# The end of a post-norm layer: order of the last tiles, low rank product apart from its transposition, last norm on POOL

## The chip, the cores and the metric

The kernel runs on one core of one Trainium2 chip. The metric is the device time of one execution in microseconds (us); lower is better. Times of the profile are counted from the start of its span. PE is the matrix engine, PEld its weight loads, DVE the vector engine, ACT the activation engine, POOL the general engine, SP the engine that issues most DMAs.

## What is computed

One transformer layer with a norm behind each half, in float32, on 2 sequences of 512 tokens and 512 channels:

```python
x = _layernorm(x + attention(x, Wq, bq, Wk, bk, Wv, bv, Wo, bo))   # 32 heads, 8 groups, D = 128, RoPE, causal softmax
x = _layernorm(x + ffn(x, ...))

def ffn(x):
    y = einsum('bth,oh->bto', x, W_base) + b_base
    z = einsum('bth,erh->bter', x, lora_A[active])                 # 4 active experts of rank 8
    contribs = einsum('bter,eor->bteo', z, lora_B[active]) * 2.0
    logits = (einsum('bth,eh->bte', x, router_W) + router_b)[..., active]
    alpha = softmax(log(domain_prior[active] + 1e-12) + logits)
    return y + einsum('bteo,bte->bto', contribs, alpha)
```

## The kernel before

The order of every instruction is written out by hand: each engine works through its own queue in the order in which the program names the instructions, and waits there for whatever an instruction needs from another engine. Attention is cut into 16 units (8 groups times 2 sequences) and each unit into four blocks of 128 query rows, which are `parts` 0 to 63. The function `slot(T)` is called once for every step T; four steps make the scores of one part. In step T stand the score of step T, the context product (`weigh`) of an earlier step, softmax steps of the three scores before, the transposition of probabilities on DVE (`blocks_transposed`), their way through DRAM (`blocks_out`, then `blocks_in` two parts later, both on SP's queue), and then whatever `put(T, ...)` has hung on that step. A context product of part p stands in step 4p + 12 (`LAG_CTX`), and ACT copies its sum out of the one PSUM bank `ctx` one step after the last (`context_out`). The output product (`wo_mm`, four heads) and `wo_out`, which adds it to the residual `x_sb`, follow.

The last 19 steps and what stands behind them also hold the second half of the layer. Its eight tiles of 128 tokens are objects of the class `Ffn`: `f0` are the four tiles of the first sequence (`fz` is the last of them), `fa` two tiles of the second, `fb` the third and `fc` the fourth. The last unit's parts come in the order 2, 3, 0, 1, so that parts 62 and 63 are short ones. A tile goes through these steps:

- `stats`, `root`, `centre`: the first norm (DVE, then Sqrt on ACT and a reciprocal on DVE, then DVE);
- `transpose`: four PE transposes into a bank `tp` and an ACT copy to `x1T`;
- `base`: x times W_base in two banks, with the low rank and router columns in the same products (4 times `base(c)`, 16 instructions); for fc, `route` does the router columns alone, 16 columns wide, and `half` the two halves of the base product later;
- `logits`, `alphas`: softmax over four experts (DVE, Exp on ACT, DVE), ending in `zs`;
- `low_rank`: PE transposes `zs` into `tz`, DVE copies that to `zT`; `finish`: PE multiplies `zT` (33 rows) with `bmT` into the base product's banks, DVE adds the residual and takes the statistics of the second norm;
- `store`: the second norm is applied (`Norm.apply`, a tensor_scalar on DVE) and SP issues the store. fc is added on PE (`ident` times x) and stored in two halves, on SP's and ACT's queue.

E is the step after the last score (256) and A is 245. The banks are QX and QY for f0[0], f0[1], fz and fb; SC and SC for f0[2], fa[0] and fc; WX and WY for fa[1]; CTX serves the contexts and some transposes; `tz` has a bank of its own.

Of the kernel before, what the change touches and what calls it, by code (L numbers as in the profile page):

```python
# [9 lines left out]
F32 = mybir.dt.float32  # L10
# [5 lines left out]
P = 128  # L16
# [13 lines left out]
def postln_layer_kernel(  # L30
# [33 lines left out]
    nc = tc.nc  # L64
    B, S, HID = x.shape
    NT = B * S // P
    TPB = S // P
    KC = HID // P
# [470 lines left out]
    def weigh(p, j):  # L539
        u, i = parts[p]  # L540
        g, b = unit(u)
        if j == 0:
            psc[p] = ps_ctx.tile([P, R, P], F32, tag="ctx", name="pc")
        nc.tensor.matmul(  # L544
            psc[p], lhsT=v_sb[g // VG, b * TPB + j][:, ts(g % VG, D)], rhs=pT[p][:, :, ts(j, P)],
            start=(j == 0), stop=(j == i))

    def context_out(p):
        ctxT[p] = work.tile([P, R, P], F32, tag="ctxT", name=f"ctxT_{p}", bufs=3)
        nc.scalar.copy(ctxT[p], psc[p])  # L550
# [73 lines left out]
    class Norm:  # L624
# [4 lines left out]
            self.rstd = pool.tile([P, n], F32, name=f"rstd_{name}")  # L629
            self.pool = pool  # L630

        def stats(self, i, *srcs):

            st = self.pool.tile([P, len(srcs), 6], F32, tag=f"st{len(srcs)}", name="st", bufs=2)
            for k, src in enumerate(srcs):
                nc.vector.bn_stats(st[:, k, :], src)  # L636
            nc.vector.bn_aggr(self.mv[:, i, :], st)

        def root(self, lo, hi):
            nc.scalar.activation(self.rstd[:, lo:hi], self.mv[:, lo:hi, 1], AF.Sqrt, bias=eps_sb)  # L640
            nc.vector.reciprocal(self.rstd[:, lo:hi], self.rstd[:, lo:hi])

        def apply(self, i, dst, src=None):
            nc.vector.tensor_scalar(
                dst, dst if src is None else src, self.mv[:, i, 0:1], self.rstd[:, i : i + 1], ALU.subtract, ALU.mult)

    class Ffn:
# [28 lines left out]
        def base(self, c):  # L676
            if c == 0:
                self.new_banks()
            for n in range(2):
                w = OH + (ARH, WX_COLS - OH)[n]  # L680
                nc.tensor.matmul(  # L681
                    self.py[n][:, :w], lhsT=self.xT[:, c, :], rhs=wbT[:, c, n, :w], start=(c == 0), stop=(c == KC - 1),
                    skip_group_check=True)
# [40 lines left out]
        def finish(self):  # L724
            for n in range(2):
                nc.tensor.matmul(  # L726
                    self.py[n][:, :OH], lhsT=self.zT, rhs=bmT[:, ts(n, OH)], start=False, stop=True,
                    skip_group_check=True)
            for n in range(2):
                nc.vector.tensor_tensor(self.y[:, ts(n, OH)], self.py[n][:, :OH], self.x[:, ts(n, OH)], ALU.add)  # L730
            self.norm2.stats(self.i, self.y)

        def half(self, n):

            if n == 0:
                self.py = [pool.tile([P, OH], F32, tag=tag, name="ph") for pool, tag in self.banks]
            py = self.py[n]
            for c in range(KC):
                nc.tensor.matmul(py, lhsT=self.xT[:, c, :], rhs=wbT[:, c, n, :OH], start=(c == 0), stop=False)
            nc.tensor.matmul(py, lhsT=ident, rhs=self.x[:, ts(n, OH)], start=False, stop=False)  # L740
            nc.tensor.matmul(py, lhsT=self.zT, rhs=bmT[:, ts(n, OH)], start=False, stop=True)

        def store(self):
            self.norm2.apply(self.i, self.y)
            nc.sync.dma_start(out=outf[ts(self.t, P), :], in_=self.y)

        def store_halves(self):
# [15 lines left out]
    def put(slot, f):  # L763
        extra.setdefault(slot, []).append(f)
# [46 lines left out]
            put(wo_from(set_units(n)[0]) - 1 + k, lambda n=n, k=k: wo_sums(n, k))  # L811


    plain_at = {}
    free = LAST + LAG_WO + 1
    for p in range(NP - 2 * TPB, NP):
# [5 lines left out]
    def slot(T):  # L822

        uq, step = divmod(T + 24, UNIT)
        kq, step = divmod(step, 8)
        now = B <= uq < NU
        if now and step != 7 and step != 4:
            q_products(uq, kq, {0: 2, 1: 6, 2: 5, 3: 7, 5: 4, 6: 3}[step])
        un, kn = (uq, 1) if kq == 0 else (uq + 1, 0)
        if B <= un < NU and step == 7:  # L830
            q_products(un, kn, 1)
        plain_q = T - T_BEGIN < UNIT and divmod(T - T_BEGIN, QB)
        if plain_q:
            r, c = plain_q
            q_mm(1, r, c, *q_banks[r])
        uk, l = divmod(T + UNIT, UNIT)
        if 0 < uk < NU and l < KC:
            k_mm(uk, l)

        gv, tv = divmod(2 * (uk - 3) + (l >= 11), NT)  # L840
        gv += 1
        new_v = 0 < gv < G // VG and (gv > 1 or tv >= 3)
        if new_v and l in (7, 8, 11, 12):
            for c in range(2):
                v_mm(gv, tv, 2 * (l in (8, 12)) + c, ps_k, "k")
        kw, sw = divmod(T - LAG_WO, 8)
        products = 0 <= kw < LAST // 8
        if products:
            wo_products(kw, sw)
        plain = plain_at.get(T)  # L850
        if plain:
            p, step_o = plain
            wo_mm(p, 2 * step_o)
            wo_mm(p, 2 * step_o + 1)
        if 0 <= T < T_END:
            score(T)
        pc, j = divmod(T - LAG_CTX, QB)
        if 0 <= pc < NP and j <= parts[pc][1]:
            weigh(pc, j)

        if now and step in (0, 2, 4, 6):
            q_copy(uq, kq, ("p1", "u2", "u3", "c21")[step // 2])
        pc, j = divmod(T - 1 - LAG_CTX, QB)
        if 0 <= pc < NP and j == parts[pc][1]:
            context_out(pc)

        if 0 <= T - 3 < T_END:
            normalise(T - 3)
        if 0 <= T - 1 < T_END:
            masked_max(T - 1)  # L870
            exponentials(T - 1)
        if products:
            wo_adds(kw, sw)
        if sw == 0 and 0 < kw <= LAST // 8:
            wo_adds(kw - 1, 8)
        if now and step in (1, 5, 7):
            q_sum(uq, kq, {1: 0, 5: 2, 7: 3}[step])
        if 0 <= T - 2 < T_END:
            reciprocals(T - 2)
        if 0 <= T - 4 < T_END:  # L880
            blocks_transposed(T - 4)
            if (T - 4) % QB == QB - 1:
                blocks_out((T - 4) // QB)
        if T % QB == 1 and 0 <= T // QB - 2 < NP:
            blocks_in(T // QB - 2)
        if 0 <= (T - LAG_WO + 1) // 8 < LAST // 8 and (T - LAG_WO + 1) % 8 == 0:
            ctx_sums((T - LAG_WO + 1) // 8)

        ur, sr = divmod(T + 24 - 7, UNIT)
        kr, sr = divmod(sr, 8)  # L890
        if B <= ur < NU and sr < 6:
            q_rope(ur, 2 * kr + (sr < 3), sr % 3)
        r, part = divmod(T - T_BEGIN - QB, QB)
        if 0 <= r < R and part < 3:
            q_rope(1, r, part)
        if 0 < uk < NU and l in (KC, KC + 1, KC + 2):
            k_rope(uk, l - KC)
        if new_v and l in (10, 14):
            v_out(gv, tv)
        if plain and step_o:  # L900
            wo_out(p)
        for f in extra.pop(T, ()):
            f()
# [74 lines left out]
    for k, f in enumerate(f0):  # L978
        put(A + (-7, -6, 0, 0)[k], f.stats)
        put(A + 1 + k // 2, f.centre)  # L980
        put(A + 3 + k // 2, lambda f=f, k=k: f.transpose(*(QX, QY)[k % 2]))
        at = A + (5, 10, 12, 100)[k]
        for c in range(KC):
            put(at + c // 2, lambda f=f, c=c: f.base(c))
        put(at + 2, lambda f=f: (f.logits(), f.alphas()))
        put(at + 3, lambda f=f: (f.low_rank(), f.finish()))
    put(A + 15, lambda: (f0[0].norm2.root(0, 3), [f.store() for f in f0[:3]]))
    put(E + 2, fa[0].stats)
    for T in range(T_PROJ, E + 7):
        slot(T)  # L990


    fz = f0[3]
# [6 lines left out]
    fa[0].norm1.root(0, 2)  # L1000
    for f in fa:
        f.centre()
    for r in range(R):
        wo_mm(NP - 2, r)
    wo_out(NP - 2)
    for j in range(2):
        weigh(NP - 1, j)
    context_out(NP - 1)
    base(fz)
    fb.stats()  # L1010
    fb.norm1.root(0, 1)
    fb.centre()
    for f in fa:
        f.transpose(*SC)
    for r in range(R):
        wo_mm(NP - 1, r)
    wo_out(NP - 1)
    fc.stats()
    fc.norm1.root(0, 1)
    fc.centre()  # L1020
    fz.logits()
    fz.alphas()
    base(fa[0])
    fb.transpose(*CTX)
    fz.low_rank()
    fz.finish()
    fa[0].logits()
    fa[0].alphas()
    base(fa[1])
    fc.transpose(*CTX)  # L1030
    fa[0].low_rank()
    fa[0].finish()
    fc.route(*CTX)
    fc.logits()
    fc.alphas()
    fa[1].logits()
    fa[1].alphas()
    base(fb)
    fc.low_rank()
    fa[1].low_rank()  # L1040
    fa[1].finish()
    fb.logits()
    fb.alphas()
    fz.norm2.root(3, 4)
    fz.store()
    fc.half(0)
    fa[0].norm2.root(0, 2)
    for f in fa:
        f.store()
    fb.low_rank()  # L1050
    fb.finish()
    fc.half(1)
    fb.norm2.root(0, 1)
    fb.store()
    fc.norm2.stats(0, *fc.py)
    fc.norm2.root(0, 1)
    fc.store_halves()

# [49 lines left out]
```

## Time and profile before

| | |
|---|---|
| median of 3 runs | 850.36 us (848.46 to 852.32) |
| the profiled execution | 850.84 us, span 849.1 us |
| mean granted PE clock | 0.993 |
| PE busy | 831.3 us, 98% of the span |
| DVE, ACT, POOL busy | 599.9, 347.2, 277.3 us |
| chain that ended last | PE 91%, DVE 5%, ACT, DMA, issue and POOL 1% each |
| last score product starts | 770.08 us |
| last PE product ends, last store issued | 843.98, 846.28 us |

In the rows of the timeline the first number is the start, the second the time on the engine, then come engine, line, operation, tiles written and read, their shapes and how many instructions were merged; in brackets stands how long the engine was idle before, and who released it. A float32 product counts as two instructions.

### The profile page before, as it was taken

How to read it: one execution, taken by the hardware profiler on the slowest of the kernel's cores; microseconds unless marked ns; L12 is line 12 of the kernel's file. 1: busy time of each engine (PE TensorE's matmuls, PEld its weight loads, DVE VectorE, ACT ScalarE, POOL GpSimd, SP SyncE). 2: the span in 40 equal slices, each digit the busy share in tenths (PEclk: the TensorE clock that was granted, in tenths of full speed). 3: DMA queues.
4: the chain of work that ended last, by engine and by line, in shares of the span. 5: the costliest groups of instructions: out<-in, count | busy, mean ns of one | idle time of the engine just before them, and what ended most of it. 6: DMA issues, size and time to landing. Idle time of an engine off the chain costs nothing.

```text
span 849.1 us, 10726 instructions
## 1 busy us (share of the span) xinstructions
PE 831.3 (98%) x3201; PEld 587.0 (69%) x3201; DVE 599.9 (71%) x1970; ACT 347.2 (41%) x996; POOL 277.3 (33%) x312
## 2 busy tenths in 40 slices
PE   9999999999999999999999999999999999999895
PEld 5567767777777777777777777777777776555463
DVE  5478977787757877686768777787768779654444
ACT  1225454535444453444343453435343445651221
POOL 6463334233332234233422134353432424000000
PEclk9999999999999999999999999999999999999997
DMA  9026536462744455462634555463626445771201
GB/s 292 31 66 190 159 97 192 106 195 71 199 112 125 149 160 157 102 192 69 195 100 126 164 159 151 134 205 84 187 77 187 136 116 166 221 218 49 86 1 62
DMA packets 84971, 116.47 MB, mean 137 GB/s; under 512 B 6581, under 2 KB 64797, under 8 KB 82866
## 3 DMA queue, kind: packets, MB, share of 16 engines
q1 hardware_dynamic: 84258, 115.50, 47.6%
q0 software_dynamic: 448, 0.14, 0.2%
q8 instruction: 25, 0.41, 0.2%
q14 instruction: 32, 0.26, 0.1%
q10 hardware_dynamic: 208, 0.15, 0.1%
HBM read 71.73 MB, written 44.04 MB: 136 GB/s over the span
## 4 chain that ended last, share of the span: by engine, by line
PE 91%; DVE 5%; ACT 1%; DMA 1%; issue 1%; POOL 1%; DVEq 0%; SPq 0%; POOLq 0%
PE pc L544 16%; PE sc L488 13%; PE qx L429 11%; PE wx L429 11%; PE pp L355 9%; PE qy L429 8%; PE wy L429 8%; PE pv L342 7%; PE py L681 3%; PE po L615 2%; PE tp L274 1%; DMA pT<-db 1%; PE py L726 1%; DVE st L636 1%; DVE wt L568 0%
## 5 line engine op out<-in xcount | busy, mean ns | idle before, releaser
L503 ACT ACTIVATE p<-sc,nmax 128x288 f32<-128x288 f32 (+15 forms) x256 | 124.2, 485 | 254.1 <-DVE nmax L496 207.7
L496 DVE CUSTOM_DVE_ANT_0 sc<-sc,maskw 128x288 f32<-128x288 f32 (+15 forms) x256 | 114.2, 446 | 154.8 <-PE sc L488 152.1
L544 PE MATMUL pc<-pT,v 128*128 128x512 f32 x320 | 165.7, 600 | 2.2 <-DMA pT<-db 1.4
L488 PE MATMUL sc<-kT,qT 128*128 128x160 f32 (+15 forms) x512 | 161.9, 398 | 1.1 <-ACT p L503 1.1
L511 ACT ACTIVATE p<-p,den 128x288 f32<-128x288 f32 (+15 forms) x256 | 133.5, 521 | 0.1
L376 POOL TENSOR_TENSOR qT<-q,t 128x512 f32<-128x512 f32 x56 | 71.0, 1268 | 188.1 <-DVE q L375 188.1
L488 PEld LDWEIGHTS sc<-kT,qT 128*128 128x128 f32 x512 | 96.8, 190 | 30.5 <-issue 14.3
L416 POOL TENSOR_TENSOR cs<-ctxT 128x256 f32<-128x256 f32 x28 | 26.5, 946 | 196.2 <-PE wy L429 109.5
L550 ACT COPY ctxT<-pc 128x512 f32<-128x512 f32 x64 | 37.4, 585 | 121.0 <-PE pc L544 121.0
L519 DVE STREAM_TRANSPOSE zt<-p 128x128 f32<-128x128 f32 (+2 forms) x192 | 81.8, 426 | 0.0
L544 PEld LDWEIGHTS pc<-pT,v 128*128 128x128 f32 x320 | 56.9, 190 | 22.4 <-issue 5.3
L355 PE MATMUL pp<-xT,wk 128*128 128x512 f32 x128 | 65.0, 593 | 0.5 <-ACT xT L275 0.5
L342 PE MATMUL pv<-wv,xT 128*128 128x256 f32 x256 | 63.6, 379 | 0.0
L429 PE MATMUL wx<-wo,ctxT 128*128 128x256 f32 x224 | 57.7, 380 | 0.4 <-DVE den L507 0.4
L429 PE MATMUL qx<-xs,wq 128*128 128x256 f32 x224 | 58.0, 381 | 0.0
L342 PEld LDWEIGHTS pv<-wv,xT 128*128 128x128 f32 x256 | 48.5, 190 | 13.4 <-issue 7.1
L521 DVE STREAM_TRANSPOSE zt<-p 128x32 f32<-128x32 f32 (+3 forms) x256 | 57.6, 225 | 0.0
L429 PEld LDWEIGHTS qx<-xs,wq 128*128 128x128 f32 x224 | 41.4, 190 | 22.3 <-issue 16.0
L429 PEld LDWEIGHTS wx<-wo,ctxT 128*128 128x128 f32 x224 | 42.4, 190 | 13.5 <-issue 7.7
L503 ACT ACTIVATION_READ_ACCUMULATOR p<-sc,nmax 128x1 f32 x256 | 49.9, 195 | 0.0
L601 DVE TENSOR_TENSOR x_sb<-wx,x_sb 128x256 f32<-128x256 f32 x112 | 47.0, 419 | 0.0
L368 DVE SCALAR_TENSOR_TENSOR t<-q,bqkT,rope_sb 64x512 f32<-64x512 f32 x56 | 43.0, 768 | 1.3
(187 smaller groups left out, 1354.7 us busy)
## 6 DMA issues: line engine op xcount, KB each, us to landing
db<-zt SPq DMA_DIRECT2D x64, 256.0 KB, 4.1
pT<-db SPq DMA_DIRECT2D x16, 1024.0 KB, 4.8
db<-zt SPq DMA_DIRECT2D x64, 192.0 KB, 3.1
pT<-db SPq DMA_DIRECT2D x16, 768.0 KB, 4.4
wq<-in_L_attn_Wq_dram SPq DMA_DIRECT2D x20, 512.0 KB, 4.6
wo<-in_L_attn_Wo_dram SPq DMA_DIRECT2D x10, 1024.0 KB, 7.6
db<-zt SPq DMA_DIRECT2D x64, 128.0 KB, 2.4
pT<-db SPq DMA_DIRECT2D x16, 512.0 KB, 4.1
```

Source lines behind the costliest of these rows:

```text
L342: nc.tensor.matmul(psq["v", gg, t], lhsT=xT[:, c, ts(t, P)], rhs=wvs[gg][0][:, c, :], start=(c == 0), stop=(c == KC - 1))
L355: nc.tensor.matmul(psq[key], lhsT=wt[:, c, cols], rhs=xT[:, c, ts(b, S)], start=(c == 0), stop=(c == KC - 1))
L376: nc.gpsimd.tensor_tensor(dst, t1[:].rearrange("p (n s) -> p n s", s=BLK), t2[:].rearrange("p (n s) -> p n s", s=BLK), ALU.add)
L429: nc.tensor.matmul(ps, lhsT=wt[:, c, :], rhs=xt[:, c, :], start=start and c == 0, stop=c == CH - 1, skip_group_check=True)
L488: nc.tensor.matmul(sc[s][:, :w], lhsT=qT[u][:, i * QB + n].rearrange("p r s -> p (r s)"), rhs=kT[u][:].rearrange("p n s -> p (n s)")[:, :w ...
L496: nc.vector.tensor_tensor_reduce(sc[s][:, :w], sc[s][:, :w], maskw[:, S - w :], -SCALE, -MASKED, ALU.add, ALU.min, nmax[s])
L503: nc.scalar.activation(ptile[s][:, :w], sc[s][:, :w], AF.Exp, bias=nmax[s], scale=-1.0, accum_out=rden[s])
L511: nc.scalar.activation(ptile[s][:, :w], ptile[s][:, :w], AF.Copy, scale=rden[s])
L519: nc.vector.transpose(z[:, :, last - i : last, n, :].rearrange("p q j s -> p j q s"), ptile[s][:, : i * P])
L521: nc.vector.transpose(z[:, : n + 1, last, n, :], ptile[s][:, i * P : w])
L544: nc.tensor.matmul(psc[p], lhsT=v_sb[g // VG, b * TPB + j][:, ts(g % VG, D)], rhs=pT[p][:, :, ts(j, P)], start=(j == 0), stop=(j == i))
L601: nc.vector.tensor_tensor(into, pw[k, bank], into, ALU.add)
```

## The change

The change touches the last steps only. `low_rank` and `finish` of a tile are put apart, with other PE work between them, and `finish` is split into the product (`finish`) and the DVE part (`add`). `Norm.apply` takes an engine, and `store` uses POOL; fc's `store_halves` stays on DVE. Part 62's context product comes one step later, part 63's behind `base(fz)`. f0[1] and f0[2] start one step later, and the stores of f0[0] to f0[2] stand behind the steps. The two `half` products of fc are cut into single steps, between which fb's `finish` is placed, and fc's statistics are taken half by half. In the tail the order of the tiles' steps is another one.

```diff
-        def apply(self, i, dst, src=None):
-            nc.vector.tensor_scalar(
+        def apply(self, i, dst, src=None, engine=nc.vector):
+            engine.tensor_scalar(
                 dst, dst if src is None else src, self.mv[:, i, 0:1], self.rstd[:, i : i + 1], ALU.subtract, ALU.mult)
...
+        def add(self):
             for n in range(2):
                 nc.vector.tensor_tensor(self.y[:, ts(n, OH)], self.py[n][:, :OH], self.x[:, ts(n, OH)], ALU.add)
             self.norm2.stats(self.i, self.y)
...
+        def half(self, n, c):
+            if n == c == 0:
                 self.py = [pool.tile([P, OH], F32, tag=tag, name="ph") for pool, tag in self.banks]
+                self.st = self.own([P, 2, 6], "st")
+            nc.tensor.matmul(
+                self.py[n], lhsT=self.xT[:, c, :], rhs=wbT[:, c, n, :OH], start=(c == 0), stop=False)
+        def half_end(self, n):
             py = self.py[n]
-            for c in range(KC):
-                nc.tensor.matmul(py, lhsT=self.xT[:, c, :], rhs=wbT[:, c, n, :OH], start=(c == 0), stop=False)
             nc.tensor.matmul(py, lhsT=ident, rhs=self.x[:, ts(n, OH)], start=False, stop=False)
             nc.tensor.matmul(py, lhsT=self.zT, rhs=bmT[:, ts(n, OH)], start=False, stop=True)
+        def half_stats(self, n):
+            nc.vector.bn_stats(self.st[:, n, :], self.py[n])
+            if n:
+                nc.vector.bn_aggr(self.norm2.mv[:, self.i, :], self.st)
         def store(self):
-            self.norm2.apply(self.i, self.y)
+            self.norm2.apply(self.i, self.y, engine=nc.gpsimd)
             nc.sync.dma_start(out=outf[ts(self.t, P), :], in_=self.y)
...
+    weigh_at = {}
+    for p in range(NP - 1):
+        for j in range(parts[p][1] + 1):
+            weigh_at.setdefault(QB * p + LAG_CTX + j + (p == NP - 2), []).append((p, j))
...
-        at = A + (5, 10, 12, 100)[k]
+    for f, at in zip(f0, (A + 5, A + 11, A + 13)):
         for c in range(KC):
             put(at + c // 2, lambda f=f, c=c: f.base(c))
         put(at + 2, lambda f=f: (f.logits(), f.alphas()))
-        put(at + 3, lambda f=f: (f.low_rank(), f.finish()))
-    put(A + 15, lambda: (f0[0].norm2.root(0, 3), [f.store() for f in f0[:3]]))
+        put(at + 3, f.low_rank)
+        put(at + 4, lambda f=f: (f.finish(), f.add()))
...
     for f in fa:
         f.centre()
+    f0[0].norm2.root(0, 3)
+    for f in f0[:3]:
+        f.store()
     for r in range(R):
         wo_mm(NP - 2, r)
     wo_out(NP - 2)
-    for j in range(2):
-        weigh(NP - 1, j)
-    context_out(NP - 1)
     base(fz)
     fb.stats()
     fb.norm1.root(0, 1)
     fb.centre()
+    for j in range(2):
+        weigh(NP - 1, j)
+    context_out(NP - 1)
     for f in fa:
         f.transpose(*SC)
+    fb.transpose(*CTX)
+    fz.logits()
+    fz.alphas()
     for r in range(R):
         wo_mm(NP - 1, r)
     wo_out(NP - 1)
     fc.stats()
     fc.norm1.root(0, 1)
     fc.centre()
-    fz.logits()
-    fz.alphas()
+    fz.low_rank()
     base(fa[0])
-    fb.transpose(*CTX)
-    fz.low_rank()
-    fz.finish()
     fa[0].logits()
     fa[0].alphas()
+    fz.finish()
+    fc.transpose(*CTX)
+    fz.add()
     base(fa[1])
-    fc.transpose(*CTX)
     fa[0].low_rank()
-    fa[0].finish()
     fc.route(*CTX)
     fc.logits()
     fc.alphas()
     fa[1].logits()
     fa[1].alphas()
-    base(fb)
+    fa[0].finish()
+    fa[0].add()
+    fa[1].low_rank()
+    for c in range(KC):
+        fb.base(c)
+        if c == 1:
+            fa[1].finish()
+            fa[1].add()
     fc.low_rank()
-    fa[1].low_rank()
-    fa[1].finish()
+    fz.norm2.root(3, TPB)
+    fa[0].norm2.root(0, 2)
+    for f in (fz, *fa):
+        f.store()
     fb.logits()
     fb.alphas()
-    fz.norm2.root(3, 4)
-    fz.store()
-    fc.half(0)
-    fa[0].norm2.root(0, 2)
-    for f in fa:
-        f.store()
+    for c in range(KC):
+        fc.half(0, c)
+    fc.half_end(0)
+    fc.half_stats(0)
     fb.low_rank()
-    fb.finish()
-    fc.half(1)
+    for c in range(KC):
+        fc.half(1, c)
+        if c == 1:
+            fb.finish()
+            fb.add()
+    fc.half_end(1)
     fb.norm2.root(0, 1)
     fb.store()
-    fc.norm2.stats(0, *fc.py)
+    fc.half_stats(1)
     fc.norm2.root(0, 1)
     fc.store_halves()
```

More of the change, by code (lines that the diff above doesn't have):

```diff
@@ L630, in __init__, with stats @@
             self.pool = pool
[L632 to L636, printed above, removed]
+        def stats(self, i, src):
+            st = self.pool.tile([P, 6], F32, tag="st", name="st", bufs=2)
+            nc.vector.bn_stats(st, src)
             nc.vector.bn_aggr(self.mv[:, i, :], st)
@@ L731, in finish @@
             self.norm2.stats(self.i, self.y)
-        def half(self, n):
-            if n == 0:
+        def half(self, n, c):
+            if n == c == 0:
                 self.py = [pool.tile([P, OH], F32, tag=tag, name="ph") for pool, tag in self.banks]
+                self.st = self.own([P, 2, 6], "st")
+            nc.tensor.matmul(
+                self.py[n], lhsT=self.xT[:, c, :], rhs=wbT[:, c, n, :OH], start=(c == 0), stop=False)
+        def half_end(self, n):
             py = self.py[n]
-            for c in range(KC):
-                nc.tensor.matmul(py, lhsT=self.xT[:, c, :], rhs=wbT[:, c, n, :OH], start=(c == 0), stop=False)
             nc.tensor.matmul(py, lhsT=ident, rhs=self.x[:, ts(n, OH)], start=False, stop=False)
             nc.tensor.matmul(py, lhsT=self.zT, rhs=bmT[:, ts(n, OH)], start=False, stop=True)
+        def half_stats(self, n):
+            nc.vector.bn_stats(self.st[:, n, :], self.py[n])
+            if n:
+                nc.vector.bn_aggr(self.norm2.mv[:, self.i, :], self.st)
         def store(self):
-            self.norm2.apply(self.i, self.y)
+            self.norm2.apply(self.i, self.y, engine=nc.gpsimd)
             nc.sync.dma_start(out=outf[ts(self.t, P), :], in_=self.y)
@@ L856, in slot @@
             score(T)
-        pc, j = divmod(T - LAG_CTX, QB)
-        if 0 <= pc < NP and j <= parts[pc][1]:
-            weigh(pc, j)
+        for part, j in weigh_at.get(T, ()):
+            weigh(part, j)
         if now and step in (0, 2, 4, 6):
             q_copy(uq, kq, ("p1", "u2", "u3", "c21")[step // 2])
-        pc, j = divmod(T - 1 - LAG_CTX, QB)
-        if 0 <= pc < NP and j == parts[pc][1]:
-            context_out(pc)
+        for part, j in weigh_at.get(T - 1, ()):
+            if j == parts[part][1]:
+                context_out(part)
         if 0 <= T - 3 < T_END:
```

## The prediction

> **What bounds the kernel now.** I read the page first for the busy shares, then the chain of waits, then the timeline of the end. TensorE (PE) is busy 831.3 of 849.1 us and holds 91% of the chain, and the diff first moves an instruction at slot A+8 (the `tz` transposition at 765.26 us). So only the last 85 us matter, and there the question is where PE stands still or runs slowly.
>
> ```profile
> PE   9999999999999999999999999999999999999895
> POOL 6463334233332234233422134353432424000000
> PEclk9999999999999999999999999999999999999997
> ...
> L376 POOL TENSOR_TENSOR qT<-q,t 128x512 f32<-128x512 f32 x56 | 71.0, 1268 | 188.1 <-DVE q L375 188.1
> ```
>
> Only the last slices have lost clock; POOL is empty there. The timeline names the holes:
>
> ```profile
> 787.67 1.12 PE L544 MATMUL pc<-pT,v 128*128 128x512 f32 x2 [0.87 <-ACT ctxT L550]
> 788.63 0.27 PE L721 MATMUL tz<-ident,zs 128*32 128x128 f32 x1
> 788.94 0.28 DVE L722 COPY zT<-tz 32x128 f32<-32x128 f32 x1 [1.04 <-PE tz L721]
> 789.36 1.10 PE L726 MATMUL py<-bmT,zT 33*128 33x256 f32 x4 [0.46 <-DVE zT L722]
> ...
> 794.58 0.52 SPq L537 DMA_DIRECT2D pT<-db  x1
> ...
> 798.75 1.98 PE L544 MATMUL pc<-pT,v 128*128 128x512 f32 x4 [1.22 <-DMA pT<-db]
> ...
> 821.02 1.96 PE L691 MATMUL zl<-wbT,x1T 128*128 128x16 f32 x16
> ...
> 825.73 0.26 DVE L712 TENSOR_TENSOR zs<-py,al 128x16 f32<-128x16 f32 x2
> ...
> 832.87 1.28 ACT L640 ACT_TABLE_LOAD   x1
> ...
> 836.26 0.27 DVE L722 COPY zT<-tz 32x128 f32<-32x128 f32 x1
> 836.59 2.00 PE L726 MATMUL py<-bmT,zT 33*128 33x256 f32 x4 [2.61 <-DVE zT L722]
> ```
>
> A reader sees transposition, copy, product with PE idle between (788.63 to 789.36); a context waiting for its bank, another for its load; and 2.61 us at the end, where fb's `zT` copy queued on DVE behind roots and three 512-wide norms. Busy time in stretches of 3.41 us shows the other loss:
>
> ```profile
> 812.80:816.21 3.41, 2.57 (x11) 1.79 (x11) 2.11 (x7) 0.58 (x1) 0.00 (x0) 1.00 0.01 2
> 819.62:823.04 3.42, 3.05 (x21) 2.69 (x22) 1.97 (x6) 0.42 (x1) 0.00 (x0) 1.00 0.02 5
> 823.04:826.45 3.41, 3.41 (x9) 2.46 (x9) 1.82 (x12) 0.78 (x4) 0.00 (x0) 0.50 0.00 0
> 833.28:836.69 3.41, 0.80 (x4) 0.28 (x3) 2.26 (x9) 1.35 (x3) 0.00 (x0) 1.00 0.17 64
> 836.69:840.10 3.41, 3.41 (x8) 2.31 (x9) 1.73 (x4) 0.07 (x1) 0.00 (x0) 0.50 0.44 167
> 840.10:843.51 3.41, 3.41 (x9) 2.31 (x8) 1.05 (x3) 0.22 (x1) 0.00 (x0) 0.50 0.20 77
> ```
>
> The second column is the stretch, then busy time of PE, PEld, DVE, ACT, POOL, then the granted clock. It halves after two poor stretches: one mostly idle, one "busy" with the 16-column router products (L691) and 33-row products only.
>
> **What is removed.** From start to start, warm, a base is 3.70 us (16 instructions), a Wo product of four heads 3.45, a context step 0.86, a low rank product (L726) 1.03, a tile's transposes 0.44, a `tz` 0.12.
> - Four pairs with nothing between (f0[0], f0[1], f0[2], fa[0]): 0.73 - 0.12 = 0.61 each, 2.44.
> - Context 62: 787.67 less (785.77 + 0.86) = 1.04. One slot later it lies behind other PE work, and ACT has copied context 61 out of the bank by then (0.56).
> - Context 63: 798.75 less (790.39 + 6.87) = 1.49. The load `pT` on SP stood behind f0's three stores, which waited for DVE. After, the stores leave SP's path, the last score transposes come some 4 us earlier on DVE (f0[1]'s adds are moved behind them), and `base(fz)` (3.70) is put ahead. I reckon landing at 790 and first use at 798.
> - fz: wait for `zs` 0.54 (behind the 1.28 table load at 810.75) and 0.62 for the pair, 1.16. fc with fa[1]: 0.53 + 0.62 = 1.15. fb: 836.59 - 833.69 - 0.12 = 2.78.
>
> Sum 10.06. Slow clock: `base(fb)` took 5.31 (822.98 to 828.29), 1.61 over; fb's product 1.92, 0.89 over; `half(1)` with its two additions 5.47 against 2.79 for `half(0)`, 2.68. Sum 5.18, which goes with the old places. Together 15.24.
>
> **What is added.** Each PE item keeps its work; I walked the four queues of the new order with the durations above.
> - Slot A+16: f0[2]'s `tz` needs a DVE chain behind f0[1]'s adds. From that product's start: 0.71 to the first sum, 0.86 adds, 0.91 statistics, 1.5 logits to `zs`, 4.1 in all; PE has 1.03 + 1.71 + 0.86 = 3.6 for it. Idle 0.5.
> - fa[1]'s `tz` (the largest). It now stands ahead of `base(fb)`, straight after fa[0]'s product. Before, route to fa[1]'s `zs` took 821.02 to 825.99 = 4.97, fc's logits coming first on DVE; that was covered by `base(fb)`. After, PE has only 1.96 of route and 1.03 of product: idle 2.0. All behind it (fb's base, halves) waits too.
> - Small ones: fa[1]'s `zT` behind fa[0]'s adds 0.2; fz's `zs` 0.1; last statistics behind fb's reciprocal 0.25. Sum of the new idle 3.1.
> - ACT table loads: alternation of Sqrt and Exp makes seven switches from here on instead of three. The row: 1.28 us, starting 0.02 after the instruction before it. At that price three of the four hide (before fc's root some 1 us spare, before fa[0]'s exponential 0.7, before fb's last root 3) and fz's makes the 0.1. The Trainium skill (ScalarE: Activation LUTs, "What ACT_TABLE_LOAD costs") speaks against the change: batch by set, about 2.66 us a switch with a drain of 1.38. No drain shows here, so I use the row; at the page's price fz's `zs` and fb's `zs` slip by 1.3 and 0.9, sum 2.2 more.
> - Norm apply on POOL: no such row. Bounds 0.49 (DVE's 1.46 for three) and 1.27 (POOL's two-input row above); I take 1.27, POOL's own. f0's three and fz's, fa's three have nothing behind them but their stores, with POOL's and SP's queues empty. fb's apply starts some 2.2 us before the last store is issued, so 1.27 hides; DVE loses 3.6 us of work, whose gain is already in the terms above. Cover ends at about 2 us.
> - `half_stats(0)` only moves earlier; separate adds are the same instructions.
>
> Warm sum: 15.24 - 3.1 = 12.1, so 850.84 - 12.1 = 838.7 us (the profiled execution's time, span 849.1 and 1.74 around it; it stands 0.48 over the median of the runs, 850.36, and I don't carry that over since the warm part is the same in any run).
>
> **The clock again.** From the end of `base(fa[1])` come 0.12 `tz`, 1.96 route, 1.03 product with 33 rows, 2.0 idle: over 5 us poorer than the stretch 819.62 to 823.04 that lost the clock. The falls at 823.04 and 836.69 lie four times 3.41 us apart; wherever such a grid falls, one stretch lies almost wholly in it. The Trainium skill (TensorE: Matmul & The Clock Gate, "Why this matters for your kernels") asks only for no idle gap over about 3 us: by it 2.0 us cost nothing, and the sum is 838.7. The row says otherwise, since the clock fell at 823.04 with PE 3.05 of 3.42 us busy. A stretch released by full work costs 1.7 less what falls into the idle time (1.2 to 1.7); the row 836.69 shows that a product of 33 rows inside it keeps it slow for another, up to 4.6 in all. I take 2.4: 841.1 us.
>
> **Rivals.**
> - Clock stays full (the page's rule): 838.7. Against it, the row 819.62.
> - Switches at the page's price or handoffs longer than reckoned: 843.3 to 846. For it, the four new loads; against it, the gap of 0.02.
> - Clock stays at half until the end: 11.4 us of PE work after the hole doubles, less 1 in the idle time: 838.7 + 10.4 = 849.1, no change. For it, two slow stretches in a row at 836.69; against it, `base(fb)` and the half products, which freed the clock at 826.45.
> - Slower: POOL's apply is far dearer than both bounds. Four stand in a row at the end. By the walk the last PE step ends 16.6 us after `base(fa[1])` (5.3 up to fa[1]'s `tz`, then 3.7, 1.2, 0.1, 2.6, 0.1, 3.6), the kernel 5.4 later (849.10 - 843.99, and 0.25), and 2.4 of slow clock make it 24.4. The applies can begin at 10.9 + 2.4, and fb's store takes 2.85 (849.10 - 846.25): 16.1 and four applies. At 6 us each that is 40.1, or 15.7 over: 856.8. The old time is passed from 4.5 us each. For it, no such instruction in the trace; against it, 1.27 for two inputs.
> - It doesn't act: `zs` is not ready at any moved `tz`, so gaps only move. That is the fa[1] case; for the others the walk shows cover.
>
> **How the numbers follow.** Forecast 0.62 (own range 839.5 to 844), full clock 0.13, dearer switches 0.09, half clock to the end 0.08, POOL 0.05, slips unseen 0.03. Faster by over 0.5% (4.2 us, about what a measurement of this kernel tells from no change): the first three, 0.84. Within: half clock and 0.02 of slips, 0.10. Slower: POOL and 0.01 of slips, 0.06. The range 837.5 to 846.5 holds the first three.
>
> **What would show it.** Right: no PE wait over 0.1 us between each `tz` and L726 but fa[1]'s; a PE idle of about 2 us before fa[1]'s `tz`, on DVE `zs`; clock 0.5 for one to two stretches from there and none at the last half; no wait on `pT`; seven table loads near 1.28 us; POOL applies near 1 us; last store about 2.8 us before the end. Wrong: POOL applies over 2 us with fb's store last, slow clock in `half(1)`, or `tz` of fz or fb waiting on ACT.

## The result, and the profile after

The changed kernel takes 840.75 us (median of 6 runs, 839.86 to 845.13) against 850.33 (6 runs, 848.46 to 854.18); the ratio is 0.9893, 95% interval 0.9862 to 0.9925. The profiled execution took 840.69 us (span 838.9) against the forecast 841.1. It has the same 3201 PE instructions, busy for 826.0 us instead of 831.3. From the page of the kernel after, its busy tenths in 40 slices:

```profile
PE   9999999999999999999999999999999999999996
POOL 6463344233332334233332334344323523300023
PEclk9999999999999999999999999999999999999998
```

POOL now works in the last slices, and the clock loses less there. The timeline of the kernel after shows what became of the holes:

```profile
782.34 0.27 PE L719 MATMUL tz<-ident,zs 128*32 128x128 f32 x1
782.45 2.01 PE L679 MATMUL py<-wbT,x1T 128*128 128x272 f32 x8
...
784.39 1.13 PE L724 MATMUL py<-bmT,zT 33*128 33x256 f32 x4
...
785.47 0.53 SPq L537 DMA_DIRECT2D pT<-db  x1
...
787.27 1.02 PE L544 MATMUL pc<-pT,v 128*128 128x512 f32 x2
...
795.51 6.43 POOL L642 TENSOR_SCALAR y<-y,mv_f,rstd_f 128x512 f32<-128x512 f32 x3 [72.41 <-DVE rstd_f L639]
...
798.61 1.88 PE L544 MATMUL pc<-pT,v 128*128 128x512 f32 x4
...
816.15 1.13 PE L724 MATMUL py<-bmT,zT 33*128 33x256 f32 x4
...
817.53 0.26 DVE L710 TENSOR_TENSOR zs<-zl,al 128x16 f32<-128x16 f32 x2
...
818.97 0.26 DVE L710 TENSOR_TENSOR zs<-py,al 128x16 f32<-128x16 f32 x2
...
819.28 0.40 PE L719 MATMUL tz<-ident,zs 128*32 128x128 f32 x1 [2.00 <-DVE zs L710]
819.47 3.32 PE L679 MATMUL py<-wbT,x1T 128*128 128x272 f32 x8
...
832.96 2.08 POOL L642 TENSOR_SCALAR y<-y,mv_f1b,rstd_f1b 128x512 f32<-128x512 f32 x1 [0.28 <-DVE rstd_f1b L639]
...
835.35 0.41 ACTq L760 DMA_DIRECT2D out_dram<-y  x1
835.49 0.38 SPq L760 DMA_DIRECT2D out_dram<-y  x1
```

Work of 1.0 us (fb) to 3.9 us (fz) stands between transposition and low rank product, and no wait is printed on the latter. Both contexts (L544) start without a wait; the load left at 785.47, not 794.58. One hole is left, 2.00 us ahead of fa[1]'s transposition (its `zs`, 818.97, stands on DVE behind fc's, 817.53), and the base product behind it is slow: 3.25 us to the next start (819.47 to 822.72) where half of a warm base takes 1.85. The norms on POOL take 2.08 us each, and SP's last store leaves behind the one for fb. In the kernel before, the norm of fb on DVE was:

```profile
840.55 0.55 DVE L644 TENSOR_SCALAR y<-y,mv_f1b,rstd_f1b 128x512 f32<-128x512 f32 x1
```

The busy table in stretches of 3.41 us (columns as in the prediction) shows the slow clock:

```profile
815.25:818.66 3.41, 2.03 (x13) 1.54 (x12) 1.35 (x9) 0.95 (x5) 0.00 (x0) 1.00 0.00 0
818.66:822.08 3.42, 2.80 (x7) 2.21 (x8) 2.20 (x9) 1.41 (x2) 0.00 (x0) 0.50 0.00 0
822.08:825.49 3.41, 3.41 (x14) 2.31 (x14) 1.73 (x4) 0.20 (x1) 0.00 (x0) 1.00 0.00 0
```

One slow stretch, against three before, and none in the last `half`.

To compare kernels without what drifts earlier, I measure each profile from the start of the last score product (`sc`, 128x256) to the end of the last PE product, and from there to the end of the span:

| profile | last score to last PE | last PE to end | sum |
|---|---|---|---|
| before | 73.9 | 5.1 | 79.0 |
| after | 63.7 | 5.9 | 69.5 |
| e1 transposition behind base | 62.7 | 7.8 | 70.5 |
| e2 norms on DVE | 65.1 | 5.3 | 70.4 |
| e3 before, contexts only | 72.7 | 5.1 | 77.7 |
| e4 before, norms on POOL | 78.5 | 7.3 | 85.8 |
| e5 hole filled, wide | 62.3 | 5.9 | 68.2 |
| e6 hole filled, thin | 70.5 | 5.8 | 76.3 |
| e7 pairs together | 65.1 | 5.9 | 71.0 |
| e8 e1 and last norm on DVE | 61.1 | 6.9 | 68.0 |
| e9 router interleaved | 60.6 | 5.1 | 65.6 |
| e10 contexts back | 67.3 | 5.8 | 73.1 |

Runs of one kernel differ by 6 us and more. Those of the kernel after, run once more (e11), go with the mean PE clock in the large: 839.66 to 841.59 us at 0.995 to 0.997, 845.99 at 0.992. So medians are read with their intervals, and effects of 1 us from the waits of the profiles.

### The profile page after: what moved, and what is told of

Same layout as the page of the kernel before. It is cut to its first block, busy times and chain, and to the rows that moved or that the text cites. A ratio compares the mean times of both kernels' runs of the same rounds, so it can differ in the third digit from the quotient of the medians.

```text
span 838.9 us, 10734 instructions
## 1 busy us (share of the span) xinstructions
PE 826.0 (98%) x3201; PEld 583.9 (70%) x3201; DVE 595.7 (71%) x1963; ACT 353.1 (42%) x1000; POOL 292.3 (35%) x319
## 4 chain that ended last, share of the span: by engine, by line
PE 92%; DVE 3%; DMA 1%; ACT 1%; POOL 1%; issue 1%; SPq 0%; DVEq 0%; POOLq 0%
PE pc L544 16%; PE sc L488 13%; PE qx L429 11%; PE wx L429 11%; PE pp L355 10%; PE qy L429 8%; PE wy L429 8%; PE pv L342 7%; PE py L679 3%; PE po L615 3%; PE tp L274 1%; PE py L724 1%; DMA x_sb<-_attn_hidden_states_dram 1%; DMA pT<-db 0%; DVE wt L568 0%
## 5 line engine op out<-in xcount | busy, mean ns | idle before, releaser
L544 PE MATMUL pc<-pT,v 128*128 128x512 f32 x320 | 165.5, 599 | 0.5 <-DMA pT<-db 0.5
L544 PEld LDWEIGHTS pc<-pT,v 128*128 128x128 f32 x320 | 57.0, 190 | 19.5 <-issue 5.7
```

The source lines that it names most:

```text
L544: nc.tensor.matmul(psc[p], lhsT=v_sb[g // VG, b * TPB + j][:, ts(g % VG, D)], rhs=pT[p][:, :, ts(j, P)], start=(j == 0), stop=(j == i))
```

## The experiments

**The hole ahead of fa[1]'s transposition (e1, e8).**

```diff
-    fa[1].low_rank()
     for c in range(KC):
         fb.base(c)
         if c == 1:
-            fa[1].finish()
-            fa[1].add()
+            fa[1].low_rank()
+    fa[1].finish()
+    fa[1].add()
     fc.low_rank()
+    fb.logits()
+    fb.alphas()
     fz.norm2.root(3, TPB)
     fa[0].norm2.root(0, 2)
     for f in (fz, *fa):
         f.store()
-    fb.logits()
-    fb.alphas()
```

> The kernel after, with fa[1]'s transposition moved behind the first half of base(fb), its product behind base(fb), and fb's logits ahead of the second norm's roots. Theory (the hole of 2.0 us ahead of that transposition costs its own length and brings on the slow clock that follows): the hole goes and the clock stays full, 2.0 and 1.4 us less than after, about 837.3 us or a ratio near 0.985. Rival 1 (the 16 column router products bring on the slow clock, not the hole): the hole goes, the slow stretch stays at base(fb), 1 to 2 us less than after. Rival 2 (the wait only moves, to fb's transposition): within 0.5 us of after.

840.82 us, ratio 0.9898 (0.9873 to 0.9923): no gain over the kernel after. The hole was gone, and PE ended 1.0 us sooner by the table. Yet in this run the clock fell all the same, now on `base(fb)` itself, where rival 1 has it, so the theory that the hole alone brings it down does not hold; and the end came later. Its timeline:

```profile
817.59 3.64 PE L679 MATMUL py<-wbT,x1T 128*128 128x272 f32 x8
...
830.61 4.13 POOL L642 TENSOR_SCALAR y<-y,mv_f1a,rstd_f1a 128x512 f32<-128x512 f32 x2
...
834.72 2.07 POOL L642 TENSOR_SCALAR y<-y,mv_f1b,rstd_f1b 128x512 f32<-128x512 f32 x1
834.76 0.39 ACTq L760 DMA_DIRECT2D out_dram<-y  x1
837.25 0.38 SPq L760 DMA_DIRECT2D out_dram<-y  x1
```

My edit put the roots behind fb's logits, so POOL's queue of four norms began later (828.56 instead of 826.48) and fb's norm waited for fa's two. SP's last store followed it at 837.25, 2.5 us behind ACT's. The next kernel has one edit more (`store` takes the engine as an argument):

```diff
     fb.norm2.root(0, 1)
-    fb.store()
     fc.half_stats(1)
+    fb.store(nc.vector)
```

> The first experiment (fa[1]'s transposition behind half of base(fb)) with one more edit: fb's last norm on DVE, behind fc's statistics, instead of POOL. Theory (the experiment's gain was eaten by POOL, whose three norms for fz and fa ended at 834.7 so that fb's store left at 836.8 and fc's first half at 837.25): the last store leaves near 834.9, 1.5 to 2.3 us less than the first experiment, 838.5 to 839.3 us. Rival (the slow stretch or PE ended it): as the first experiment, 840.8.

839.18 us, ratio 0.989 (0.9873 to 0.9906). The two ran beside different runs of before (849.28 and 848.47), so half of the 1.6 us between the medians is not theirs; the table shows 0.9 less from the last PE product to the end. SP's last store left at 833.52, 0.83 behind ACT's (fa's norm on POOL still stands before it in SP's queue): POOL held the end up in e1, and does a little here. In this profile the clock stayed full to the last product over the same PE order as e1's. What differs is where the stretches of 3.41 us fall. In e1 the clock fell at 818.01, and the 3.41 us ahead of that hold 0.6 us of base products; in e8 it fell at 833.33, behind the last product, and the stretches counted back from there that begin at 812.86 and 816.27 hold 1.3 and 2.6 us of them. At full clock the edit to the hole is worth 1.2 us (61.1 in the table against 62.3 of e5, which keeps the hole's time and fills it); 0.6 of its 2.0 comes back as a wait on fb's `zT`.

**What brings the clock down (e5, e6).** Both put unused products into the hole (the comments have what e6 has instead):

```diff
+    fill = ps_q.tile([P, 2 * P], F32, tag="qx", name="fill")
+    for _ in range(4):                                   # e6: range(16)
+        nc.tensor.matmul(fill[:, :256], lhsT=ident, rhs=wbT[:, 0, 0, :256], start=True, stop=True)   # e6: 16 columns
     fa[1].low_rank()
```

> The kernel after, with four products of 256 columns (128 rows, 1.7 us in all, result unused) put into the 2.0 us hole ahead of fa[1]'s transposition. Theory A (the clock falls after a stretch of about 3.4 us with little array work, whether PE is idle in it or has thin products): the stretch now has 1.7 us of full products and the clock stays full or falls less often; base(fb)'s first half takes 1.85 instead of 3.25 us, 1.0 to 1.4 us less than after. Theory B (the router products alone bring it down): slow clock and time as after, 840.7.

> The kernel after, with sixteen products of 16 columns (some 1.9 us of busy PE, little array work, result unused) put into the same hole. Theory A: thin products count as idle, the clock falls as in after, and the time is that of after within 0.5 us. Theory C (the clock falls for idle time alone): PE is busy, so it stays full and 1.0 to 1.4 us are gained.

Wide: 839.23 us, ratio 0.989 (0.9871 to 0.9909), which alone can't be told from the kernel after, but its profile has no slow stretch before the last product and 1.4 less in the table's first column, and the mean clock of its four runs is 0.996 to 0.999 (the kernel after: 0.992 to 0.997). Where the grid falls has a say here too: from the end of `base(fa[1])` to the filling there are 2.96 us of thin products (814.35 to 817.31), as many as ahead of `base(fb)` in e1, where the clock fell. Thin: 843.94 us, 0.994 (0.9924 to 0.9957), and in the profiled run, the slowest of its four (847.34; the others 843.37 to 844.24), the clock was down for four stretches. The timeline and the busy table of the thin one:

```profile
817.01 5.79 PE L1060 MATMUL fill<-wbT,ident 128*128 128x16 f32 x32
822.64 0.37 PE L719 MATMUL tz<-ident,zs 128*32 128x128 f32 x1
...
814.65:818.06 3.41, 3.41 (x27) 2.99 (x26) 1.19 (x8) 0.57 (x3) 0.00 (x0) 1.00 0.00 0
818.06:821.47 3.41, 3.41 (x20) 3.41 (x19) 2.19 (x8) 1.79 (x4) 0.00 (x0) 0.55 0.00 0
821.47:824.88 3.41, 3.41 (x13) 2.79 (x13) 0.28 (x1) 0.00 (x0) 0.00 (x0) 0.50 0.00 0
824.88:828.30 3.42, 3.42 (x9) 2.14 (x7) 0.23 (x1) 0.00 (x0) 0.00 (x0) 0.50 0.00 0
828.30:831.71 3.41, 3.41 (x9) 2.19 (x8) 1.49 (x4) 1.37 (x2) 0.00 (x0) 0.50 0.00 0
```

PE (second number) is busy throughout, and the clock falls nevertheless. Theory A holds in kind: thin products count for little, and C, idle time alone, falls. A was too mild in size: it expected the time of the kernel after. One part of that is a slip in the reckoning: a float32 product is two instructions, so the sixteen are 32 (x32 above). The router's 16 instructions take 1.79 us (814.16 to 815.95 in this profile), so by that pace 32 take an estimated 3.6 us at full clock and not 1.9, longer than the hole. The other part is the clock: they took 5.63 us (817.01 to 822.64), kept it down and pushed everything behind them. The two kernels ran side by side, 4.7 us apart, of which an estimated 1.6 (3.6 less the hole's 2.0) would be the filling itself. B falls with the wide one and with e8, where the clock stays full over the same router products.

**Norms on POOL (e2, e4).**

```diff
         def store(self):
-            self.norm2.apply(self.i, self.y, engine=nc.gpsimd)
+            self.norm2.apply(self.i, self.y)
```

> The kernel after, with every store's norm on DVE as before. Theory (POOL's 2.08 us are off the path but for the last store, and DVE's time is what the move buys): fz's and fa's three norms (1.55 us) now stand ahead of fb's logits, whose cover is 0.7, so fb's transposition waits 0.9 more; fb's own norm delays the last statistics by 0.3; the last stores leave 0.5 earlier. Sum 0.5 to 1.0 us slower than after. Rival (POOL sets the end, since a norm took 2.08 us there against 0.5 on DVE): 0.5 us or more faster than after.

841.95 us, ratio 0.9916 (0.9891 to 0.9941); the interval overlaps that of the kernel after, so the time alone doesn't decide. The profile does for its parts:

```profile
831.14 0.28 PE L719 MATMUL tz<-ident,zs 128*32 128x128 f32 x1 [0.59 <-DVE zs L710]
```

fb's transposition waits 0.59 us for `zs`, no such wait stands in the kernel after, and from the last PE product to the end it is 5.3 instead of 5.9. The two nearly cancel; the rest of the table's difference is a second slow stretch in this profile. Both theories were right on one term; neither is large.

> The kernel before, with the stores' norms on POOL and nothing else changed. Theory (a norm takes 2.08 us on POOL, and f0's three stand ahead of the load of context 63 on SP): that load leaves 6.2 instead of 1.5 us after the roots, PE waits some 4.7 us longer and runs slowly behind that (1.7 to 3.4), while fb's transposition is copied 1.55 us earlier and the clock may stay full at the end (up to 3.6 back). Sum 1 to 6 us slower than before, ratio 1.001 to 1.007. Rival (moving the norm off DVE is what made the change faster): 1.5 us or more faster than before.

The same edit the other way round, on the kernel before: 856.89 us, ratio 1.0073 (1.0041 to 1.0104). Its timeline:

```profile
793.73 6.37 POOL L644 TENSOR_SCALAR y<-y,mv_f,rstd_f 128x512 f32<-128x512 f32 x3 [69.69 <-DVE rstd_f L641]
...
800.69 0.52 SPq L537 DMA_DIRECT2D pT<-db  x1
...
804.84 3.78 PE L544 MATMUL pc<-pT,v 128*128 128x512 f32 x4 [6.19 <-DMA pT<-db]
```

The slower norms stand ahead of the load in SP's queue, PE waits 6.19 us where it waited 1.22, and the context product after that takes twice its time. This was expected, at the upper end of the range (1.007) or just over it. Moving the norm off DVE is not what made the change faster; it needed the new order.

**The contexts (e3, e10).** The first is the kernel before with the contexts' and f0's stores' new places (norm on DVE), the second the kernel after with the contexts in the old ones:

```diff
-            weigh_at.setdefault(QB * p + LAG_CTX + j + (p == NP - 2), []).append((p, j))
+            weigh_at.setdefault(QB * p + LAG_CTX + j, []).append((p, j))
...
     wo_out(NP - 2)
+    for j in range(2):
+        weigh(NP - 1, j)
+    context_out(NP - 1)
     base(fz)
...
-    for j in range(2):
-        weigh(NP - 1, j)
-    context_out(NP - 1)
```

> The kernel before, with one part of the change alone: context 62 one step later, context 63 behind base(fz), f0's second norm and its three stores (still on DVE) behind the steps. Theory (both context waits go and nothing takes their place): 1.04 and 1.49 us less than before, about 847.8, ratio 0.997. Rival (the time comes back at the wait for fz's zs or at fb's transposition): no change. The clock's slow stretches at the end may fall otherwise and move either by 2 us.

849.61 us, ratio 0.9999 (0.9979 to 1.0018): no difference by time, but the interval is wide enough to hide the 1.3 us that the table shows (77.7 against 79.0). By the profile the wait on the load is gone, and the wait for the bank has turned into another, the one on `zs` of f0[2]:

```profile
787.04 0.29 PE L721 MATMUL tz<-ident,zs 128*32 128x128 f32 x1 [1.16 <-DVE zs L712]
...
789.37 0.52 SPq L537 DMA_DIRECT2D pT<-db  x1
...
800.34 1.88 PE L544 MATMUL pc<-pT,v 128*128 128x512 f32 x4
```

> The kernel after, with the last two contexts in their old places (62 one step earlier, 63 ahead of base(fz)). Theory (with f0's stores off SP's path and the score transposes earlier, load and bank are ready anyway: the load left at 785.5 against a use at 794.9, the copy of context 61 ended at 783.1): no wait of PE on either, at most f0[2]'s zs is waited for 0.9 longer in the place of the context step; 0 to 0.9 us slower than after. Rival (the move of the contexts itself earns the 2.5 us that the prediction gave it): 1.5 us or more slower, with waits on ctxT or pT of over 0.5 us.

842.39 us, ratio 0.9905 (0.9877 to 0.9933), with three slow stretches in its profile (10.2 us long), so the time is of little use. The waits are: none on the bank, none on `pT` although context 63 is ahead of `base(fz)` again (796.85), and one on f0[2]'s `zs`, where none is printed in the kernel after:

```profile
790.32 0.28 PE L719 MATMUL tz<-ident,zs 128*32 128x128 f32 x1 [0.96 <-DVE zs L710]
```

From the start of the last score product to fa's transposes (L274) it takes 31.80 us here and 30.94 in the kernel after. So the contexts' new places earn 0.9 us, as cover for that `zs`. The wait on the load did not need them: with f0's stores off SP's path the load leaves at 789.37 in e3 instead of 794.58, and with the 4.2 us that it took before (794.58 to 798.75) it would be there at an estimated 793.5, ahead of 797.26 (790.39 and 6.87), where PE was done with the product before it.

**The pairs (e7).**

```diff
-        put(at + 3, f.low_rank)
-        put(at + 4, lambda f=f: (f.finish(), f.add()))
+        put(at + 3, lambda f=f: (f.low_rank(), f.finish(), f.add()))
```

> The kernel after, with the low rank product of f0[0], f0[1] and f0[2] put back directly behind its transposition (same step, adds with it). Theory (each pair with nothing between costs 0.61 us of PE): PE waits on zT three times, 1.5 to 2.2 us slower than after, about 842.5. Rival (these waits only shift PE against the softmax of the last parts, or f0[2]'s later transposition waits less for zs): within 0.5 us of after.

843.27 us, ratio 0.9917 (0.9892 to 0.9943), 2.5 us over the kernel after by the medians with overlapping intervals. The profile has three waits of 0.46 on `zT`; the one of f0[2]:

```profile
789.33 1.10 PE L724 MATMUL py<-bmT,zT 33*128 33x256 f32 x4 [0.46 <-DVE zT L720]
```

The first pair (764.13) lies ahead of the last score product. The other two make the way from there to fa's transposes 1.1 us longer (32.07 against 30.94), which is two times 0.61 less a little. The rest of the 1.4 in the table's first column is the clock: there is one slow stretch, as in the kernel after, but none of it falls into the hole. The theory holds in the profile; the time agrees but does not decide.

**A version that beats both (e9, and e12 beside e11).** From fa[0]'s transposition on, with `route` cut into its two halves:

```diff
     fa[0].low_rank()
-    fc.route(*CTX)
-    fc.logits()
-    fc.alphas()
     fa[1].logits()
     fa[1].alphas()
+    fb.base(0)
     fa[0].finish()
+    fb.base(1)
     fa[0].add()
+    fc.route_half(0, *CTX)
+    fz.norm2.root(3, TPB)
+    fa[0].norm2.root(0, 1)
+    for f in (fz, fa[0]):
+        f.store()
+    fb.base(2)
     fa[1].low_rank()
+    fb.base(3)
+    fc.route_half(1, *CTX)
+    fb.logits()
+    fb.alphas()
+    fa[1].finish()
+    fc.logits()
+    fc.alphas()
...
+    fc.low_rank()
+    fb.low_rank()
+    fa[1].add()
     fc.half_end(0)
...
+    fb.finish()
+    fb.add()
     for c in range(KC):
         fc.half(1, c)
-        if c == 1:
-            fb.finish()
-            fb.add()
     fc.half_end(1)
     fb.norm2.root(0, 1)
-    fb.store()
     fc.half_stats(1)
+    fb.store(nc.vector)
```

> The kernel after with the tail from fa[0]'s transposition on in another order: fa[1]'s logits ahead of fc's, the four steps of base(fb) spread between fa[0]'s product and the two halves of fc's router products, fb's transposition and product ahead of fc's second half, fa[1]'s sums behind the copies of both factors, the norms of fz and fa[0] early on POOL, fb's on DVE. Theory A (no stretch of 3.4 us with little array work is left): the clock stays full to the end, no PE wait over 0.3 us after base(fa[1]), last product some 15 us after it, about 836.5 us, ratio near 0.984. Rival (DVE, with all statistics in its last 5 us, becomes what ends last): 838 to 839.5.

> The interleaved order once more. Theory (no poor stretch is left, so nothing depends on where the grid falls): 836.4 to 837.7, a narrower scatter than the kernel after (under 2 us), about 3.5 us less than it. Rival (the first look was luck of the grid): some runs over 839 with a mean clock under 0.997.

> The kernel after once more, beside the interleaved order on the same chip. Theory (its scatter is the number of slow clock stretches behind the hole, one or more by where the 3.41 us grid falls): most runs near 840.7, some 3 to 5 us higher with a lower mean clock, ratio 0.988 to 0.991. Rival (the scatter is another's, such as DMA): times not ordered by the mean clock.

e9: 837.43 us, ratio 0.9863 (0.9846 to 0.988). e12: 837.04 (836.1 to 839.62), 0.9847 (0.982 to 0.9873), where the kernel after on the same chip had 840.92 (839.66 to 845.99), 0.9894 (0.9865 to 0.9923). The timeline of e9 shows thin and wide products in turn:

```profile
814.97 1.09 PE L679 MATMUL py<-wbT,x1T 128*128 128x272 f32 x4
815.99 1.13 PE L725 MATMUL py<-bmT,zT 33*128 33x256 f32 x4
817.04 1.19 PE L679 MATMUL py<-wbT,x1T 128*128 128x272 f32 x4
818.07 0.96 PE L690 MATMUL zl<-wbT,x1T 128*128 128x16 f32 x8
818.88 1.17 PE L679 MATMUL py<-wbT,x1T 128*128 128x272 f32 x4
...
825.35 0.29 PE L720 MATMUL tz<-ident,zs 128*32 128x128 f32 x1 [0.37 <-DVE zT L721]
```

In the profile of e9 the clock is full to the last product and the longest PE wait behind `base(fa[1])` is 0.37 us, on `zT`. The gain is 3.9 us by the medians of e11 and e12. The order changes several things at once: by the table 3.1 us of the gain lie ahead of the end of the last product and 0.8 behind it, and no run divides them further. One run of five, 839.62 at a mean clock of 0.996, is higher, so the scatter is 3.5 us and not under 2: the rival's luck of the grid is smaller, not gone.

## Why the prediction was right

Step by step, from the profiles:

- **The pairs.** 0.61 each; the waits are gone in the kernel after, and e7 brings three back at 0.46 of idle, two of them worth 1.1 us. Right.
- **fz, fc with fa[1], fb (1.16, 1.15, 2.78).** No PE wait is left at fz, fc or fb in the profile after (fa[1]'s is the new hole below). No experiment puts one of these back alone, so their sizes are read from the profile before only.
- **Context 62, 1.04.** Right in the sum, for a partly wrong reason. Alone, the move turns the wait into one of 1.16 on f0[2]'s `zs` (e3). In the new order the old place would have no bank wait (e10): what counts there is the cover of `zs`, 0.9.
- **Context 63, 1.49.** Gone. Of its three reasons, the stores off SP's path are enough by the estimate under e10, and `base(fz)` ahead of it is not needed (e10). The load left at 785.5, and PE came to it at 798.6.
- **New hole at fa[1], 2.0.** 2.00, on DVE `zs`, as written. f0[2]'s was 0.26 (788.39 less 787.27 and 0.86) instead of 0.5; the terms of its DVE chain sum to 3.98 and not the 4.1 that the prediction has, and it took 3.95 (784.39 to 788.34).
- **Table loads.** Seven in the profile, 1.28 each; where the next instruction is ready it starts 0.02 behind (802.60 to 803.90). The Trainium skill's drain (ScalarE: Activation LUTs, "What ACT_TABLE_LOAD costs") would by the prediction's estimate have held fz's transposition back 1.3 us; it began at 805.10 with no wait printed. The row was the right choice.
- **Clock.** The mechanism was right: the hole, the router and the 33-row product lost it in spite of a gap under 3 us. Its size was 1.4 us in this profile where I took 2.4, since 0.6 of the one stretch fell into the hole. The rule of the Trainium skill that the prediction set aside (TensorE: Matmul & The Clock Gate, "Why this matters for your kernels": no idle gap over about 3 us) does not cover this case: in e6 the clock falls with no gap at all.
- **POOL, the term that was mis-sized.** I took 1.27 us a norm, as its upper bound too; it is 2.08. The step that failed is the bound: a row of a two-input add was taken to cover an operation with one input and two scalars for each partition. The cover was put at about 2 us, so the result was spared by little: from the last PE product to the end it is 5.85 instead of 5.12, which I had put at 0.25 more. With the norms on DVE it is 5.33 (e2), so some 0.5 goes with POOL: SP's last store, behind fb's, leaves at 835.49, only 0.14 after ACT's, but takes 2.3 us to land, where SP's last store took 1.7 in the kernel before and in e2. That the store of fb just ahead of it is what delays it is likely, not shown.
- **The sum.** Predicted against the profiled execution: 9.74 less. Measured: 79.0 - 69.5 = 9.5 after the last score, and 0.7 ahead of it (770.08 to 769.39), 10.2. f0[0]'s pair lies in the latter, but two profiles of the kernel after differ there by as much (769.39, and 768.63 in e11). That the forecast came within 0.4 us is in part luck: the clock was put 1.0 too dear and POOL 0.5 too cheap, and two of the six runs, at a mean clock of 0.992, took 844.22 and 845.13.

Of the rivals, full clock to the end is what e5 shows would happen with other content in the hole, not what did. The slower one (POOL) is real where the norms stand ahead of something: e4 is slower by 0.73%, some 6 us.

## What to carry to other kernels

A short chain from PE through another engine and back is hidden by placing any ready work between, but look at the queue of the middle engine: of eight such chains one kept its 2.0 us because another tile's softmax stood first there. When work goes to a slower engine, look at what waits behind it in the store queue, not at its busy share. Between groups of thin products put wide ones: the clock here followed how much of some 3.4 us was filled with wide products, not whether PE was busy.

## What was not expected of the hardware

- A `tensor_scalar` with two per-partition scalars over 128x512 float32 took 2.08 us on POOL and 0.55 on DVE.
- With PE busy without a break the clock halved after a stretch of 16-column and 33-row products (e6, 814.65 to 818.06), and stayed down for 13.7 us, four times 3.41. At half clock, two stretches with base products in 2.0 of their 3.41 us (from 821.47 and 824.88) did not bring it back, and one with 2.9 did (from 828.30). Whether columns, rows or both count is not separated by these runs.
- The slow stretches come in lengths of 3.41 us (3.4, 10.2, 13.7 us in the profiles of after, e10 and e6). Where that grid falls against the program isn't the same in each run (e1 and e8). That a run of the kernel after near 845 us has several of them is argued from its mean clock; the two profiled runs (840.69 and 840.18) have one. What sets the grid is left open.
